# Last tiles of two experts side by side in TensorE's columns, and narrow tiles turned as 80 rows

## The chip, the core and the metric

The kernel runs on one core of a Trainium2 chip. The metric is the device time of one execution in microseconds; the time given is the median of three runs. The engines are named as in the profile: PE (TensorE), DVE (VectorE), ACT (ScalarE), POOL (GpSimd), SP (SyncE, which issues DMAs here).

## The reference

A graph layer with a mixture of experts, then a residual and a layer norm, over 12500 nodes of 256 features. Each node goes to its best 2 of 64 experts; the part of the reference around the change is this:

```python
h1 = gelu(einsum('ecd,edh->ech', h, w1) + b1[:, None, :], approximate=False)   # 256 -> 512
h2 = einsum('ech,ehd->ecd', h1, w2) + b2[:, None, :]                           # 512 -> 256
y_s = where(valid[:, None], h2.reshape(E * CAP, D)[slot], 0.0)
core = zeros((N, D)).at[tok_s].add(g_s[:, None] * y_s)                         # both experts of a node
```

`h` holds the rows of the nodes that an expert was given (at most CAP = 1024 for each), `g_s` the gate of a node for the expert. All is float32.

## The kernel before

The program has stages that follow each other: degrees and ordering of the edges, sums over edges, graph convolution and choice of experts, the experts, and the two normalisations. The change is in the stage of the experts.

**The work of the stage.** The experts are ordered by the number of their nodes, and `TOKENS` holds for each place in that order a bound in units of 16 rows. `parts` cuts each expert's rows into parts of at most four tiles of 128 rows (P); the last tile of an expert may have 16, 32, 48, 64, 80, 96 or 112 rows. There are 83 parts: the smallest expert first, then the others from the largest down.

**One part q.** Its steps, with the lines of the profile:

- `begin(q)`: when the part is an expert's first, registers are loaded with the expert's number, the expert's table of rows is copied (`tables`, L1762), and `load` issues the DMAs of its weights on SP (`w`, L1614, 1026 KB, and `bb`); `gather` (L1638) then issues on POOL one indirect DMA per tile, which fetches the rows into `xg` (16 buffers). The weights have three buffers.
- `turned(q)`: `gates_of` (L1682, DVE) makes the gates from two further columns of the gathered rows; `turn` transposes the tiles on PE into `xtp` (L1653) and copies them on DVE to `xT` (L1658).
- `hidden(q)`: eight matmuls `hp` (L1667) and four Gelu on ACT (L1671).
- `outputs(q)`: for each tile four matmuls into `yp` (L1694; two PSUM buffers), each with a tile of `h1` as the stationary operand, so that a tile of r rows uses r of PE's 128 columns. In the trace each float32 matmul shows as two records, a transpose as one. DVE adds the bias (L1699) and multiplies by the gate (L1700) into `yo` (six buffers), and POOL issues the indirect DMA that adds the rows to `z_d` (L1701). Scatter-adds of one expert are declared free of each other; one of another expert waits for the landing of those before it.

**What sets the order.** PE's order is the program's (`manual_schedule` for PE): hidden(q), transposes of part q+1, products of part q. Gathers are called three parts ahead (`AHEAD`). On the other engines a scheduler places the instructions, by priorities of its own; each engine then works through its queue in order.

```python
h1 = hidden(given[i][0], xT, m)
if q + AHEAD < len(parts):
    begin(q + AHEAD)
if q + 1 < len(parts):
    xT = turned(q + 1)
outputs(*given[i], table(q), gate.pop(q), h1, m, f"expert{i}")
```

Of the kernel before, what the change touches and what calls it, by code (L numbers as in the profile page):

```python
# [8 lines left out]
F32 = mybir.dt.float32  # L9
# [5 lines left out]
ALU = mybir.AluOpType  # L15
# [4 lines left out]
P = 128  # L20
N = 12500
D = 256
H = 512
E = 64
# [72 lines left out]
def last_node(g):  # L97
# [12 lines left out]
]  # L110
RPE = CAP // P
NSLOT = E * RPE
WROW = 2 * H + 4 * D + 4
# [8 lines left out]
def gnn_moe_kernel(  # L122
# [1478 lines left out]


    with ExitStack() as stack:
        wp = stack.enter_context(tc.tile_pool(name="w", bufs=3))
        one = stack.enter_context(tc.tile_pool(name="x_one", bufs=1))
        two = stack.enter_context(tc.tile_pool(name="x_two", bufs=2))
        ps1 = stack.enter_context(tc.tile_pool(name="x_ps1", bufs=1, space=PSUM))
# [11 lines left out]
        def overfull():  # L1619
# [8 lines left out]
            V.tensor_reduce(some, room, axis=AX.X, op=ALU.add)  # L1628
            V.tensor_copy(over_n, some)

        def gather(at, m):

            xg = []
            for k in range(0, m, P):
                r = min(P, m - k)
                k //= P
                g = two.tile([P, D2], F32, name="xg", bufs=16)
                GP.indirect_dma_start(  # L1638
                    out=g[:r],
                    out_offset=None,  # L1640
                    in_=x2_d,
                    in_offset=bass.IndirectOffsetOnAxis(ap=at[:r, 0, k : k + 1], axis=0),
                )
                xg.append(g[:r])
            return xg

        def turn(xg):

            xtp = ps1.tile([P, 2, 4 * P], F32, name="xtp")
            for k, g in enumerate(xg):  # L1650
                r = g.shape[0]
                for c in range(2):
                    T.transpose(  # L1653
                        xtp[:, c, k * P : k * P + r], g[:, c * P : (c + 1) * P], ident[:r, :r]
                    )
            m = k * P + r
            xT = two.tile([P, 2, 4 * P], F32, name="xT")
            V.tensor_copy(xT[:, :, :m], xtp[:, :, :m])  # L1658
            return xT
# [17 lines left out]
        def gates_of(xg, second):  # L1677
# [7 lines left out]
                )  # L1685
            return gate

        def outputs(w, bb, at, gate, h1, m, group):
            w2 = w[:, 2 * H : 2 * H + 4 * D].rearrange("p (c d) -> p c d", d=D)
            for k in range(-(-m // P)):  # L1690
                r = min(P, m - k * P)
                yp = ps2.tile([P, D], F32, name="yp")
                for j in range(4):
                    T.matmul(  # L1694
                        yp[:r], h1[:, j, k * P : k * P + r], w2[:, j],
                        start=j == 0, stop=j == 3,
                    )
                yo = two.tile([P, D], F32, name="yo", bufs=6)
                V.tensor_add(yo[:r], yp[:r], bb[:r])  # L1699
                V.tensor_scalar_mul(yo[:r], yo[:r], gate[:r, k : k + 1])  # L1700
                st = GP.indirect_dma_start(  # L1701
                    out=z_d,
                    out_offset=bass.IndirectOffsetOnAxis(
                        ap=at[:r, 1, k : k + 1], axis=0
                    ),
                    in_=yo[:r],
                    in_offset=None,
                    compute_op=ALU.add,
                )
                if group:  # L1710
                    tc.declare_no_dep(st.ins, group=group, reason="no node has an expert twice")
                    tc.add_to_no_dep_group(group, st.ins)


        parts = []
        for i in [E - 1, *range(E - 1)]:
            n = -(-TOKENS[i] * TU // P)
            k = -(-n // 4)
            b = 0
            for j in range(k):  # L1720
                m = (n - b + k - j - 1) // (k - j)
                parts.append((i, b, min(m * P, TOKENS[i] * TU - b * P)))
                b += m
        AHEAD = 3
        xg, given = {}, {}

        def begin(q):
            i, b, m = parts[q]
            if b == 0:
                k = 0 if i == E - 1 else i % REGS  # L1730
                if k == 0:
                    n = 1 if i == E - 1 else min(REGS, E - 1 - i)
# [14 lines left out]
                    given["regs"] = regs, columns  # L1747
                regs, columns = given["regs"]
                columns_of[i] = columns[k]
                sort_slots(i, 0)  # L1750
                if q >= AHEAD:
                    sort_slots(i, 1)
                given[i] = load(regs[k])
            xg[q] = gather(table(q), m)

        columns_of = {}

        def sort_slots(i, which):

# [6 lines left out]
        def table(q):  # L1766
            i, b, m = parts[q]
            return sorted_[:, :, i * RPE + b : i * RPE + b + 4]

        def turned(q):  # L1770
            i, b, m = parts[q]
            gate[q] = gates_of(xg[q], snd_sorted[:, i * RPE + b : i * RPE + b + 4])
            return turn(xg.pop(q))

        gate = {}
        snd_sorted = one.tile([P, NSLOT], F32)
        with tc.manual_schedule(engines={mybir.EngineType.PE}):
            for q in range(AHEAD):
# [6 lines left out]
            for q, (i, b, m) in enumerate(parts):  # L1785
                if q >= 6 and q % 4 == 2 and (q - 6) // 4 < len(LOADS):
                    t0, n = LOADS[(q - 6) // 4]
                    r = rows(t0)
                    nc.sync.dma_start(xs[:r, t0 : t0 + n], part_of(x, t0, n))
                h1 = hidden(given[i][0], xT, m)  # L1790
                if q + AHEAD < len(parts):
                    begin(q + AHEAD)
                if q + 1 < len(parts):
                    xT = turned(q + 1)
                outputs(*given[i], table(q), gate.pop(q), h1, m, f"expert{i}")
                if q == 16:
                    overfull()


        with tc.If(nc.values_load(over_n[0:1, 0:1]) > 0):  # L1800
# [5 lines left out]
            with tc.For_i(0, E, 1) as e:  # L1806
# [5 lines left out]
                for b in range(0, RPE, 4):  # L1812
                    ab = at[:, :, b : b + 4]
                    g = gather(ab, 4 * P)
                    gb = gates_of(g, second[:, b : b + 4])
                    outputs(w, bb, ab, gb, hidden(w, turn(g), 4 * P), 4 * P, None)


    with ExitStack() as stack:
# [191 lines left out]
```

## Time and profile before

| | |
|---|---|
| median of three runs | 3584.51 us (3563.84 to 3585.21) |
| the profiled execution's own time | 3578.72 us |
| its span, first to last instruction | 3576.8 us |
| mean granted PE clock over the span | 0.829 |
| busy, share of the span | PE 71%, DVE 50%, ACT 22%, POOL 61% |
| matmuls `yp` (L1694) | 1928 records, 436.3 us busy |
| matmuls `hp` (L1667) | 1328 records, 392.3 us busy |
| gathers `xg` (L1638) on POOL | 241, mean 972 ns |
| scatter-adds `z_d` (L1701) on POOL | 241, mean 1556 ns |

The busy share is an average over stages with different limits. In a row of a group, the numbers behind the count are busy time and the mean duration of one instruction; matmuls overlap, so that the mean of one is longer than the distance between two. A row in order of time gives start, length, engine, line, operation, count, and in brackets how long the engine had been idle and what ended that. L numbers are lines of the kernel.

### The profile page before, as it was taken

How to read it: one execution, taken by the hardware profiler on the slowest of the kernel's cores; microseconds unless marked ns; L12 is line 12 of the kernel's file. 1: busy time of each engine (PE TensorE's matmuls, PEld its weight loads, DVE VectorE, ACT ScalarE, POOL GpSimd, SP SyncE). 2: the span in 40 equal slices, each digit the busy share in tenths (PEclk: the TensorE clock that was granted, in tenths of full speed). 3: DMA queues.
4: the chain of work that ended last, by engine and by line, in shares of the span. 5: the costliest groups of instructions: out<-in, count | busy, mean ns of one | idle time of the engine just before them, and what ended most of it. 6: DMA issues, size and time to landing. Idle time of an engine off the chain costs nothing. (4 is left out here: it accounts for less than half of the span.)

```text
span 3576.8 us, 40049 instructions
## 1 busy us (share of the span) xinstructions
PE 2531.0 (71%) x11797; PEld 1893.4 (53%) x11797; DVE 1800.6 (50%) x7368; ACT 798.8 (22%) x1975; POOL 2175.5 (61%) x2095
## 2 busy tenths in 40 slices
PE   2526075566776667676766666677699999999966
PEld 2415043455555555554555444454377876677856
DVE  3729454355555465655555435467543333333358
ACT  2416301122111122212221111111111221122246
POOL 7250776666666666666666666665367777777610
PEclk6657566778887878897878777788899999999988
DMA  8450853444554555555544444444555666676764
GB/s 259 128 189 6 309 203 95 158 145 144 143 150 146 141 147 168 146 147 157 155 144 122 142 117 122 119 135 124 159 115 122 134 135 146 155 177 173 197 196 144
DMA packets 313919, 538.03 MB, mean 150 GB/s; under 512 B 47274, under 2 KB 233102, under 8 KB 305502
## 3 DMA queue, kind: packets, MB, share of 16 engines
q0 software_dynamic: 119360, 266.30, 28.9%
q1 hardware_dynamic: 180795, 256.19, 23.0%
q10 hardware_dynamic: 13539, 12.90, 1.2%
q8 instruction: 97, 1.59, 0.2%
q14 instruction: 128, 1.05, 0.1%
HBM read 431.02 MB, written 105.28 MB: 150 GB/s over the span
## 5 line engine op out<-in xcount | busy, mean ns | idle before, releaser
L938 POOL DMA_INDIRECT ring<-h_d,src_col x1416 | 1372.4, 969 | 711.8 <-issue 387.2
L952 PE MATMUL p<-ring,o 128*128 128x258 f32 x2832 | 902.0, 450 | 213.2 <-issue 89.7
L952 PEld LDWEIGHTS p<-ring,o 128*128 128x128 f32 x2832 | 600.4, 224 | 389.2 <-issue 214.9
L930 DVE TENSOR_SCALAR o<-lane,rel 128x128 f32<-128x128 f32 x1416 | 356.1, 297 | 402.7 <-remote 160.3
L1701 POOL DMA_INDIRECT z_d<-yo,tables x241 | 375.0, 1556 | 129.8 <-issue 58.0
L1694 PE MATMUL yp<-w,h 128*128 128x256 f32 (+7 forms) x1928 | 436.3, 381 | 0.8 <-DVE tables L1762 0.8
L1667 PE MATMUL hp<-xT,w 128*128 128x384 f32 (+22 forms) x1328 | 392.3, 449 | 9.4 <-issue 9.4
L1694 PEld LDWEIGHTS yp<-w,h 128*128 128x128 f32 (+7 forms) x1928 | 336.8, 179 | 71.0 <-issue 7.6
L1638 POOL DMA_INDIRECT xg<-x_d,tables x241 | 234.3, 972 | 183.7 <-PE xtp L1653 88.2
L1671 ACT ACTIVATE h<-hp,w 128x384 f32<-128x384 f32 (+21 forms) x332 | 178.7, 539 | 682.0 <-PE hp L1667 673.1
L1667 PEld LDWEIGHTS hp<-xT,w 128*128 128x128 f32 x1328 | 248.0, 192 | 134.1 <-issue 61.0
L1506 ACT ACTIVATE again<-again,factor 128x256 f32<-128x256 f32 x180 | 82.4, 501 | 670.3 <-issue 363.2
L986 ACT COPY s<-p 128x258 f32<-128x258 f32 x118 | 43.8, 371 | 814.8 <-PE p L952 450.0
L1658 DVE COPY xT<-xtp 128x672 f32<-128x672 f32 (+21 forms) x83 | 70.8, 853 | 305.6 <-PE xtp L1653 297.2
L1699 DVE TENSOR_TENSOR yo<-yp,bb 128x256 f32<-128x256 f32 (+7 forms) x241 | 102.0, 423 | 224.1 <-PE yp L1694 154.2
L285 POOL DMA_INDIRECT early<-in_x,src_col x130 | 135.0, 1038 | 102.4 <-DMA early_d<-early 56.3
L567 PE MATMUL deg<-o_hi,o_lo 128*128 128x98 bf16 x1254 | 107.3, 254 | 122.8 <-issue 83.8
L1481 PE MATMUL q<-r_out,tables 128*128 128x98 f32 x360 | 66.8, 315 | 150.4 <-DVE tables L1489 55.9
L1027 PE MATMUL q<-ident,s 128*128 128x128 f32 x236 | 58.9, 337 | 158.0 <-DVE tables L1489 67.5
L222 DVE TENSOR_TENSOR o_hi<-lane_b,hi 128x2450 bf16<-128x2450 bf16 (+1 forms) x67 | 95.1, 1419 | 145.8 <-remote 106.2
L565 ACT ACTIVATE s_lo<-lane_b,nb 128x128 bf16<-128x128 bf16 x396 | 121.8, 388 | 192.9 <-remote 126.7
L567 PEld LDWEIGHTS <-o_lo 128*128 128x128 bf16 x1254 | 87.5, 125 | 140.1 <-issue 91.2
(367 smaller groups left out, 3503.5 us busy)
## 6 DMA issues: line engine op xcount, KB each, us to landing
w<-in_wpack SPq DMA_DIRECT2D x64, 1026.0 KB
again<-early_d SPq DMA_DIRECT2D x90, 256.0 KB
ring<-h_d,src_col POOLq DMA_INDIRECT x1416
early_d<-early SPq DMA_DIRECT2D x65, 256.0 KB
tables<-h_d SPq DMA_DIRECT2D x104, 128.0 KB
acc<-acc_d SPq DMA_DIRECT2D x14, 896.0 KB
acc<-in_x SPq DMA_DIRECT2D x12, 1024.0 KB
x_d<-y SPq DMA_DIRECT2D x47, 258.0 KB
```

Source lines behind the costliest of these rows:

```text
L285: GP.indirect_dma_start(out=t[:, c % 2], out_offset=None, in_=x, in_offset=bass.IndirectOffsetOnAxis(ap=src_col[:, MC + c : MC + c + 1], a ...
L565: S.activation(s_lo[:, i], lane_b, AF.Sign, bias=nb[:, k - k0, i : i + 1])
L567: T.matmul(deg, o_lo[:, i], o_hi[:, i], start=c + i == 0, stop=False)
L930: o_last[u] = V.tensor_scalar(o_of[u][:, j], lane, rel[:, c : c + 1], None, op0=ALU.is_equal)
L938: i = GP.indirect_dma_start(out=r[:, k, :D], out_offset=None, in_=h_d, in_offset=bass.IndirectOffsetOnAxis(ap=src_col[:, c : c + 1], axis=0),)
L952: i = T.matmul(p_of[g], o_of[v][:, n], r[:, k], start=j == 0, stop=j == GR - 1)
L1638: GP.indirect_dma_start(out=g[:r], out_offset=None, in_=x2_d, in_offset=bass.IndirectOffsetOnAxis(ap=at[:r, 0, k : k + 1], axis=0),)
L1667: T.matmul(hp[:, :m], w1[:, c, j * P : (j + 1) * P], xT[:, c, :m], start=c == 0, stop=c == 1,)
L1671: S.activation(h1[:, j, :m], hp[:, :m], AF.Gelu, bias=w[:, 2 * H + 4 * D + j : 2 * H + 4 * D + j + 1],)
L1694: T.matmul(yp[:r], h1[:, j, k * P : k * P + r], w2[:, j], start=j == 0, stop=j == 3,)
L1699: V.tensor_add(yo[:r], yp[:r], bb[:r])
L1701: st = GP.indirect_dma_start(out=z_d, out_offset=bass.IndirectOffsetOnAxis(ap=at[:r, 1, k : k + 1], axis=0), in_=yo[:r], in_offset=None, c ...
```

## The change

Of the experts whose last tile has at most 64 rows (`SIDE`), each is paired with the next such expert (`PAIR_OF`): eleven pairs. The second of a pair is moved directly behind the first, and its parts are reversed, so that the two parts that hold the last tiles follow each other. The first of these two parts computes its full tiles only and keeps its last tile's operands. At the second part, `pair_of_outputs` puts both last tiles into one `yp` tile, the first at rows 0 and the second at row 64, and alternates their matmuls: one of the first, one of the second, four times. Only then does `begin(q + AHEAD)` run, with its gathers pinned in program order, and the second part's full tiles come behind the last of these gathers.

A tile of fewer than 80 rows (`WHOLE`) is gathered and transposed as 80 rows; the copy to `xT` still takes only the part's own rows. The weights have four buffers, and the registers are loaded in groups that follow the new order.

```diff
+SIDE = P // 2
+WHOLE = SIDE + 16
+PAIR_OF = {}
+for _i, _n in enumerate(TOKENS[: E - 2]):
+    if 0 < _n * TU % P <= SIDE:
+        _open = [_k for _k, _v in PAIR_OF.items() if _v is None]
+        PAIR_OF.update({_open[0]: _i} if _open else {_i: None})
+PAIR_OF = {_k: _v for _k, _v in PAIR_OF.items() if _v is not None}
...
-        wp = stack.enter_context(tc.tile_pool(name="w", bufs=3))
+        wp = stack.enter_context(tc.tile_pool(name="w", bufs=4))
...
-                r = min(P, m - k)
+                r = max(WHOLE, min(P, m - k))
...
+                if last_gather.get("pin"):
+                    tc.keep_in_program_order(i)
+                last_gather["i"] = i.ins
...
+        def pair_of_outputs(two_of):
+
+            yp = ps2.tile([P, D], F32, name="yp")
+            sides = [yp[i * SIDE : i * SIDE + m % P] for i, (_, _, _, _, _, m, _) in enumerate(two_of)]
+            for j in range(4):
+                for side, (w, bb, at, gate, h1, m, group) in zip(sides, two_of):
+                    products(side, m % P, w, h1, m // P * P, j)
+            for i, (side, (w, bb, at, gate, h1, m, group)) in enumerate(zip(sides, two_of)):
+                r = m % P
+                add_to_nodes(
+                    side, r, bb[i * SIDE : i * SIDE + r], at, gate, m // P, group
+                )
...
+        order = [E - 1]
+        for i in range(E - 1):
+            if i not in order:
+                order += [i, *([PAIR_OF[i]] if i in PAIR_OF else [])]
...
+            parts += of[::-1] if i in PAIR_OF.values() else of
+        pair_at = {}
+        for q, (i, b, m) in enumerate(parts[1:], 1):
+            if PAIR_OF.get(parts[q - 1][0]) == i:
+                assert 0 < m % P <= SIDE and 0 < parts[q - 1][2] % P <= SIDE
+                pair_at[q] = q - 1
...
-                if q + AHEAD < len(parts):
+                if q not in pair_at and q + AHEAD < len(parts):
                     begin(q + AHEAD)
                 if q + 1 < len(parts):
                     xT = turned(q + 1)
-                outputs(*given[i], table(q), gate.pop(q), h1, m, f"expert{i}")
+                mine = (*given[i], table(q), gate.pop(q), h1, m, f"expert{i}")
+                if q in pair_at:
+                    pair_of_outputs([kept.pop(pair_at[q]), mine])
+                if q in pair_at or q in pair_at.values():
+                    if q not in pair_at:
+                        kept[q] = mine
+                    mine = (*mine[:5], m // P * P, mine[6])
+                if q in pair_at:
+                    last_gather["pin"] = True
+                    begin(q + AHEAD)
+                    last_gather["pin"] = False
+                    with tc.issue_after(last_gather["i"]):
+                        outputs(*mine)
+                else:
+                    outputs(*mine)
```

`products` holds the matmul of `outputs`, and `add_to_nodes` its add, multiplication and scatter-add, both as they were.

More of the change, by code (lines that the diff above doesn't have):

```diff
@@ L1629, in overfull @@
             V.tensor_copy(over_n, some)
+        last_gather = {}
         def gather(at, m):
@@ L1693, in outputs @@
                 for j in range(4):
[L1694 to L1708, printed above, removed]
-                )
-                if group:
-                    tc.declare_no_dep(st.ins, group=group, reason="no node has an expert twice")
-                    tc.add_to_no_dep_group(group, st.ins)
+                    products(yp[:r], r, w, h1, k * P, j)
+                add_to_nodes(yp[:r], r, bb[:r], at, gate, k, group)
+        def pair_of_outputs(two_of):
[8 more added lines that the diff above has]
+                    side, r, bb[i * SIDE : i * SIDE + r], at, gate, m // P, group
+                )
+        order = [E - 1]
+        for i in range(E - 1):
+            if i not in order:
+                order += [i, *([PAIR_OF[i]] if i in PAIR_OF else [])]
         parts = []
-        for i in [E - 1, *range(E - 1)]:
+        for i in order:
             n = -(-TOKENS[i] * TU // P)
```

50 lines of the change are left out of this document (33 added, 17 removed).

## The prediction

> **What bounds the kernel now.** I read the page first, then PE's waits and busy time in the stretch of the experts, then the chain that ended last, then the three queues (PE, DVE, POOL) in order of time.
>
> ```profile
> span 3576.8 us, 40049 instructions
> PE 2531.0 (71%) x11797; PEld 1893.4 (53%) x11797; DVE 1800.6 (50%) x7368; ACT 798.8 (22%) x1975; POOL 2175.5 (61%) x2095
> ...
> 2562.00:3429.00 867.00, 857.13 (x3734) 638.63 (x3734) 318.12 (x985) 180.00 (x333) 599.54 (x473) 0.99 0.65 151
> ...
> PE hp L1667 <- issue: 9.4, 2, 8.8
> PE yp L1694 <- DVE tables L1762: 0.8, 1, 0.8
> ```
>
> The change touches only the stage of the experts, from 2562 to 3429 us: the built programs of before and after hold the same instructions in the same order ahead of it and behind it. In this stage the columns of the window are PE, PEld, DVE, ACT, POOL: PE is busy 857.13 of 867 us, and its waits sum to 10.2 us, all at the start. So a microsecond that PE saves here is a microsecond of the kernel, and a wait put on PE costs its full length. POOL is busy 599.54 us (69%), DVE 318 us (37%).
>
> ```profile
> 3430.93 1.53 POOL z_d L1701
> ...
> 3432.79 3.70 DMA z_d<-yo,tables
> 3436.51 0.37 SPq L1852
> ```
>
> The chain says how the stage ends: the last scatter-add into z_d is issued at 3432.79, lands 3.70 us later, and only then do the loads of the next stage start. A late POOL at the end is on the path too.
>
> **Why PE never waits now: POOL's lead.**
>
> ```profile
> POOL xg L1638 <- PE xtp L1653: 87.3, 63, 2.5
> DVE gate L1682 <- DMA xg<-x_d,tables: 4.0, 6, 1.0
> ...
> 3185.78 0.94 POOL L1638 DMA_INDIRECT xg<-x_d,tables  x1 [0.30 <-issue]
> 3187.02 1.00 POOL L1638 DMA_INDIRECT xg<-x_d,tables  x1 [0.30 <-issue]
> 3188.32 1.64 POOL L1701 DMA_INDIRECT z_d<-yo,tables  x1 [0.30 <-issue]
> 3190.26 1.57 POOL L1701 DMA_INDIRECT z_d<-yo,tables  x1 [0.30 <-DVE yo L1699]
> 3192.14 1.46 POOL L1701 DMA_INDIRECT z_d<-yo,tables  x1 [0.30 <-issue]
> ...
> 3190.66 0.47 DVE L1682 SCALAR_TENSOR_TENSOR gate<-snd_sorted,xg 128x1 f32<-128x1 f32 x3
> 3195.15 0.89 DVE L1658 COPY xT<-xtp 128x704 f32<-128x704 f32 x1 [4.02 <-PE xtp L1653]
> 3196.91 0.42 DVE L1699 TENSOR_TENSOR yo<-yp,bb 128x256 f32<-128x256 f32 x1 [0.86 <-DMA z_d<-yo,tables]
> ```
>
> POOL's gathers mostly wait for a free xg buffer (87.3 us): POOL runs as far ahead as sixteen buffers allow. Therefore the gates on DVE, which read the gathered rows, find them landed: 4.0 us of waiting in the whole stage, all at its start. This matters because the scheduler puts gates early in DVE's queue: in the built program of before, behind the adds of part q stand the gates of part q+4, and only then the xT copy of part q+2 and the yo adds of part q+1. DVE works in order, so a gate whose rows are late holds that copy and those adds.
>
> **The change, part by part.**
>
> *Gathers behind the pair (the costliest edit).* For the eleven parts that end a pair, begin(q+3) is called after the pair's outputs, its gathers are pinned in program order, and the remaining outputs come after them. The scheduler kept the early gates. Around the first pair (parts 12 and 13; gN is the gates of part N, XN its xT copy) the built queues read:
>
> ```
> POOL: S12.2  S13.2  G16 x3  S13.0 S13.1  G17 x2  G18 x3  G19 x3  S14.0
> DVE:  X14  +12.2 +13.2 *12.2 *13.2  +13.0 +13.1 (*)  g16 x3  g17 x2  X15  +14.0
> PE:   pair 12|13, 13.0 13.1, hidden 14, turn 15, 14.0 14.1 14.2
> ```
>
> Before, G16 and G17 stood ahead of S11. Now they stand behind S13.2, while g17 still stands ahead of +14.0. PE has two yp buffers, so product 14.2 waits for +14.0. From the end of the pair on PE: adds and multiplications until S12.2 can go 1.4 us (three DVE rows of 0.35 to 0.42 and the signals); S13.2 is of another expert than S12.2 and waits for its landing, s; then POOL's issue spacing, 1.88 us for a scatter and 1.27 for a gather (from the rows above). For s:
>
> ```profile
> 3213.19 1.43 POOL L1701 DMA_INDIRECT z_d<-yo,tables  x1 [0.31 <-issue]
> ...
> 3221.22 1.63 POOL L1701 DMA_INDIRECT z_d<-yo,tables  x1 [1.83 <-DMA z_d<-yo,tables]
> ...
> 2552.15 1.11 POOL L1638 DMA_INDIRECT xg<-x_d,tables  x1 [40.81 <-DVE tables L1762]
> ...
> 2559.72 0.22 DVE L1682 SCALAR_TENSOR_TENSOR gate<-snd_sorted,xg 128x1 f32<-128x1 f32 x1 [6.54 <-DMA xg<-x_d,tables]
> ```
>
> s is bounded by 3.7 us (the chain, little traffic) and 7.7 (3213.19 to the end of the wait before 3221.22); I take 5.0, since the pair's end frees a weight buffer and so starts a 1 MB load at that moment. A gather's landing after POOL's part of it is bounded by 0 and 6.5 us (2553.26 to 2559.72, three weight loads under way); I take 2.3, what the chain's scatter shows (3.70 less its 1.44 on POOL).
>
> Sum for this pair: 1.4 + 5.0 + 1.88 (S13.2) + 3 x 1.27 + 2 x 1.88 + 2 x 1.27 - 0.3 + 2.3 = 20.4, and gate, X15 and +14.0 with signals 1.7: 22.1 us. PE in that time has two products tiles 3.46, hidden(14) 5.16, turn 0.65, two tiles 3.46 (rows below): 12.7. Stall: 9.4 us. With n gathered tiles, r remaining tiles, and PE's hidden+turn h, the stall is 8.5 + 1.27 n + 0.15 r - h, less 0.9 where the copy isn't behind the gates:
>
> | pair ends with part | n | r | h | stall |
> |---|---|---|---|---|
> | 13 | 5 | 2 | 5.8 | 9.4 |
> | 17 | 5 | 1 | 5.8 | 8.3 |
> | 35 | 6 | 1 | 5.8 | 9.6 |
> | 39 | 8 | 3 | 7.8 | 11.4 |
> | 46 | 7 | 3 | 6.4 | 11.5 |
> | 48 | 6 | 3 | 6.0 | 10.6 |
> | 50 | 6 | 2 | 5.8 | 10.6 |
>
> Together 71 us. For the last four pairs (64, 66, 68, 70), which follow each other, three gathers stand ahead of the copy X(q+2): 1.4 + 5.0 + 1.88 + 3.8 - 0.3 + 2.3 + 1.3 = 15.4 against 3.46 + 4.1 + 0.6 + 3.46 = 11.6 on PE: 3.8 us; and, in the first three, the next gates hold the adds that free yp, some 2.7 us more. Together 22 us. No engine hides this: PE is the bound.
>
> *What an idle PE does to its clock.*
>
> ```profile
> 2576.00:2580.00 4.00, 0.20 (x1) 0.51 0.41 101
> ...
> 2579.80 8.67 PE L1667 MATMUL hp<-xT,w 128*128 128x512 f32 x16 [8.76 <-issue]
> ...
> 2969.37 7.13 PE L1667 MATMUL hp<-xT,w 128*128 128x512 f32 x16
> ```
>
> After the one idle time of 8.76 us the granted clock (the third number from the right in a row of the window, here 0.51) was half, and sixteen matmuls took 8.67 instead of 7.13 us: 1.5 us. Seven stalls of this length: +10.5 us (bounds 0 and 15).
>
> *PE's own savings.* Each row starts where PE began the group; the time to the next row's start is its cost.
>
> ```profile
> 2885.90 0.52 PE L1653 MATMUL xtp<-ident,xg 128*128 128x128 f32 x4
> 2886.26 5.38 PE L1694 MATMUL yp<-w,h 128*128 128x256 f32 x24
> 2891.48 2.98 PE L1667 MATMUL hp<-xT,w 128*128 128x208 f32 x16
> ...
> 2894.95 3.62 PE L1694 MATMUL yp<-w,h 128*128 128x256 f32 x16
> 2898.41 5.32 PE L1667 MATMUL hp<-xT,w 128*128 128x384 f32 x16
> 2903.57 0.65 PE L1653 MATMUL xtp<-ident,xg 128*128 128x128 f32 x4
> 2904.14 5.45 PE L1694 MATMUL yp<-w,h 128*128 128x256 f32 x24
> 2909.43 2.76 PE L1667 MATMUL hp<-xT,w 128*128 128x192 f32 x16
> ...
> 2948.14 3.74 PE L1694 MATMUL yp<-w,h 128*128 128x256 f32 x16
> 2951.80 5.43 PE L1667 MATMUL hp<-xT,w 128*128 128x384 f32 x16
> 2957.07 0.60 PE L1653 MATMUL xtp<-ident,xg 128*128 128x128 f32 x4
> ```
>
> Turning 128+80 rows and the products behind it took 0.36 + 5.22 us, 128+64 rows 0.57 + 5.29: a tile of up to 64 rows costs 0.28 us more than one of 80. 24 such tiles are now turned as 80 rows: -6.7 us. Products of 128+80 rows took 3.46 us and the hidden layer behind them 5.16; of 128+32 rows 3.66 and 5.27: a narrow tile costs 0.31 us for going into PE's narrow columns and out. A record of a product costs 3.46/16 = 0.216 us, and each matmul is two.
>
> No row shows two products side by side. In the built program, five pairs keep one column width (two at 64 columns, three at 32); six alternate between a 64-wide and a 32-wide tile at every matmul. For the five, if the second record of one side overlaps the first of the other, 16 records take 9 slots: 7 x 0.216 = 1.51 saved, and one way in and out, 0.31: 1.82 each, -9.1. Bounds: 0.31 (no overlap) and 1.82. For the six I take that each of the seven inner changes of width costs half of 0.31: +1.05 - 0.31 = +0.74 each, +4.4. Bounds: +0.74 and -1.82. I choose the upper end because the only changes of width that the trace has all cost time. PE's own: -6.7 - 9.1 + 4.4 = -11.4.
>
> The Trainium skill, "TensorEngine Tiling (Array Packing)", Key Properties, says that a change of the tiling mode, not merely of the tile, drains TensorE. By it the six pairs gain nothing; without it all eleven would overlap, and this term would be -27 instead of -11.4. The trace has the change between 128 and 32 or 64 columns alone, not that between 64 and 32.
>
> *The stage's end.* Behind the last pair the built POOL queue has nine gathers ahead of S71.0: 11.4 us late; ten parts of two scatters then need about 5.7 us each on POOL (2 x 1.88 and the landing) against some 6.7 on PE, so most is made good: +4 us (0 to 11).
>
> *At nothing:* the 944 further rows that are gathered (POOL's time is per instruction), the register loads for the reordered experts (SP and DVE have room), the weight load that begin(q+3) also issues (on SP it waits for its buffer before and after), and the fourth weight buffer (PE never waited for w; the loads start a part earlier).
>
> Sum: 71 + 22 + 10.5 - 11.4 + 4 = +96 us on the profiled execution's own time, 3578.72 us (span 3576.8 and 1.9 around it): **3674 us**. That execution is 5.8 us under the median of the runs, well within their spread.
>
> **The rivals.**
> 1. *POOL's lead suffices* (not slower). If the gathers of q+3 and q+4 land before g(q+4) holds anything, no stall arises; 4.0 us of gate waits now speak for it, the queue above against it. It needs 9 us less per pair, more than s and both landings at their least give back (some 4). Then only PE's own counts: -11 to -27, 3552 to 3567 us.
> 2. *All eleven pairs overlap* (the six too): -27 instead of -11.4, 3658 us.
> 3. *The change doesn't do what it says: none overlaps.* The five lose 1.51 each: 3682 us.
> 4. *Slow landings:* s at 7.7 and gathers at 5 us under the weight loads: 11 x (2.7 + 2.7) more, 3733 us.
>
> **How the numbers follow.** Forecast 0.54, rival 1 0.10, rival 2 0.12, rival 3 0.10, rival 4 0.12; 0.02 is left for a gain that I don't see. Range: s at 3.7 takes 14 us off, gather landings at nothing 25, no clock loss 10, rival 2 15; nearly all of it: 3614 us. Upwards s and landings at two thirds of rival 4, with no overlap, and the median above the profiled execution: 3728 us. A measurement of this kernel tells about 1% (36 us) from no change. Faster by more needs more than all that PE can save: 0.02. Within 1% is rival 1: 0.10. Slower is the forecast with the three others: 0.88.
>
> **What would show it.** Right: PE's waits in the stage hold yp on DVE seven times at 8 to 12 us and hp on DVE's xT near the end, gates on DVE wait for the gathers some 100 us, and POOL's scatter waits 2 to 6 us on z_d eleven times. The granted clock halves behind each. Wrong: gates that don't wait, or yp records of a six-pair that start together. The forecast falls if PE stays busy over 95% of the stage.

## The result, and the profile after

The changed kernel takes 3700.31 us in the median of six runs (3684.30 to 3709.65), the kernel before 3576.98 us in the runs beside it. The ratio is 1.036, with a 95% interval of 1.031 to 1.041: the change costs about 123 us.

The page of the changed kernel, its span and its busy times:

```profile
span 3682.5 us, 40034 instructions
PE 2554.4 (69%) x11797; PEld 1911.4 (52%) x11797; DVE 1800.8 (49%) x7368; ACT 798.9 (22%) x1975; POOL 2187.6 (59%) x2095
```

The work is the same to within a per cent, and yet the span is 105.7 us longer, so the time went into waiting. Windows by stage of the changed kernel, and in a second block the earlier stages of the one before (the columns behind the length are the busy times of PE, PEld, DVE, ACT and POOL, the granted clock, the DMA share and GB/s):

```profile
0.00:2534.00 2534.00, 1587.64 (x7373) 1180.34 (x7373) 1373.55 (x6046) 524.37 (x1467) 1585.37 (x1619) 0.76 0.51 150
2534.00:3537.00 1003.00, 878.10 (x3738) 648.52 (x3738) 319.91 (x996) 179.80 (x333) 599.22 (x475) 0.94 0.58 132
3537.00:3682.00 145.00, 88.66 (x686) 82.53 (x686) 107.37 (x327) 94.77 (x175) 2.98 (x2) 0.84 0.56 179
```

```profile
0.00:2559.00 2559.00, 1583.86 (x7373) 1171.90 (x7373) 1373.37 (x6046) 524.00 (x1467) 1570.91 (x1618) 0.77 0.49 148
```

PE's stage of the experts, from its first transposition to its last product, took 869.0 us before and takes 1002.5 now: 133.5 more. The stages ahead of it, which the change doesn't touch, were 25.6 us shorter in this execution; that is why the spans differ by less than the stage does, and why the experiments below are read by the stage.

What PE waits for in the stage, and what DVE and POOL wait for (total, number of times, longest; `...` marks rows left out, here and below):

```profile
PE yp L1702 <- DVE yo L1706: 61.5, 12, 12.1
PE hp L1679 <- DVE xT L1670: 26.3, 4, 7.6
PE yp L1702 <- issue: 20.1, 9, 12.2
...
PE yp L1702 <- ACT h L1683: 5.8, 1, 5.8
...
DVE gate L1694 <- DMA xg<-x_d,tables: 191.1, 67, 12.8
...
POOL xg L1648 <- PE xtp L1666: 37.4, 31, 3.2
POOL z_d L1708 <- DMA z_d<-yo,tables: 19.7, 7, 5.8
```

PE's waits were 10.2 us behind the stage's first transposition; now those four kinds alone are 113.7. ("issue" names no releaser; the one wait of 12.2 us among these nine ends, like the others, right behind late gates and an add on DVE.) DVE's gates wait 191 us for gathered rows, where they waited 4. POOL waits for a free xg buffer 37 us instead of 87: it has lost its lead.

The first pair (parts 12 and 13) in order of time:

```profile
2717.52 1.43 POOL L1708 DMA_INDIRECT z_d<-yo,tables  x1 [7.76 <-DVE yo L1707]
...
2722.43 1.35 POOL L1708 DMA_INDIRECT z_d<-yo,tables  x1 [3.48 <-issue]
2724.08 1.01 POOL L1648 DMA_INDIRECT xg<-x_d,tables  x1 [0.30 <-issue]
...
2726.95 0.22 DVE L1694 SCALAR_TENSOR_TENSOR gate<-snd_sorted,xg 128x1 f32<-128x1 f32 x1 [6.49 <-DMA xg<-x_d,tables]
2727.91 1.64 POOL L1708 DMA_INDIRECT z_d<-yo,tables  x1 [0.30 <-issue]
...
2731.75 1.02 POOL L1648 DMA_INDIRECT xg<-x_d,tables  x1 [0.30 <-issue]
2733.07 0.95 POOL L1648 DMA_INDIRECT xg<-x_d,tables  x1 [0.30 <-issue]
...
2734.70 0.22 DVE L1694 SCALAR_TENSOR_TENSOR gate<-snd_sorted,xg 128x1 f32<-128x1 f32 x1 [4.65 <-DMA xg<-x_d,tables]
...
2736.13 0.21 DVE L1694 SCALAR_TENSOR_TENSOR gate<-snd_sorted,xg 80x1 f32<-80x1 f32 x1 [1.22 <-DMA xg<-x_d,tables]
2736.27 0.95 DVE L1670 COPY xT<-xtp 128x768 f32<-128x768 f32 x1
...
2737.14 0.41 DVE L1706 TENSOR_TENSOR yo<-yp,bb 128x256 f32<-128x256 f32 x1
...
2737.60 3.78 PE L1702 MATMUL yp<-w,h 128*128 128x256 f32 x8 [8.72 <-DVE yo L1706]
```

Read from the top: the scatter-add of part 12's last tile, then part 13's, held until the first has landed, 4.9 us behind it (the row says "issue", but POOL's sequencer waits there for the semaphore, the signal of landing, of the first one's DMA, whose last update came at 2721.68). Then the three gathers of part 16, part 13's full tiles, and the gathers of part 17 at 2731.75 and 2733.07. Their gates on DVE come at 2734.70 and 2736.13. Behind these gates in DVE's queue stand the xT copy and the add that frees the yp buffer, and PE's product starts right behind that add, 8.7 us idle. The chain is the one of the built queue.

Behind the stop the clock is down; a window that begins inside the stop has a granted clock of 0.51 (third number from the right), and the mean of the whole stage fell from 0.99 to 0.94:

```profile
2731.00:2741.00 10.00, 3.40 (x8) 2.78 (x9) 2.67 (x7) 0.00 (x0) 7.56 (x9) 0.51 0.45 94
```

### The profile page after: what moved, and what is told of

Same layout as the page of the kernel before. It is cut to its first block, busy times and chain, and to the rows that moved or that the text cites. A ratio compares the mean times of both kernels' runs of the same rounds, so it can differ in the third digit from the quotient of the medians.

```text
span 3682.5 us, 40034 instructions
## 1 busy us (share of the span) xinstructions
PE 2554.4 (69%) x11797; PEld 1911.4 (52%) x11797; DVE 1800.8 (49%) x7368; ACT 798.9 (22%) x1975; POOL 2187.6 (59%) x2095
## 5 line engine op out<-in xcount | busy, mean ns | idle before, releaser
L960 PEld LDWEIGHTS p<-ring,o 128*128 128x128 f32 x2832 | 608.1, 227 | 375.8 <-issue 182.1
L1702 PE MATMUL yp<-w,h 128*128 128x256 f32 (+7 forms) x1928 | 454.3, 394 | 87.5 <-DVE yo L1706 61.5
L1679 PE MATMUL hp<-xT,w 128*128 128x384 f32 (+22 forms) x1328 | 398.8, 455 | 36.2 <-DVE xT L1670 26.3
L1683 ACT ACTIVATE h<-hp,w 128x384 f32<-128x384 f32 (+19 forms) x332 | 178.5, 539 | 815.2 <-PE hp L1679 712.8
L1706 DVE TENSOR_TENSOR yo<-yp,bb 128x256 f32<-128x256 f32 (+6 forms) x241 | 101.8, 423 | 213.4 <-PE yp L1702 166.7
L1670 DVE COPY xT<-xtp 128x768 f32<-128x768 f32 (+18 forms) x83 | 70.7, 852 | 261.4 <-PE xtp L1666 207.2
L293 POOL DMA_INDIRECT early<-in_x,src_col x130 | 144.8, 1114 | 77.3 <-issue 36.9
L1489 PEld LDWEIGHTS q<-r_out,tables 128*128 128x128 f32 x360 | 63.6, 232 | 188.6 <-issue 75.0
L1313 PE MATMUL tab<-at,vals 128*128 128x512 bf16 x392 | 135.4, 433 | 29.2 <-DVE vals L1299 17.2
L1497 DVE SCALAR_TENSOR_TENSOR tables<-lane,high,q 128x98 f32<-128x98 f32 x180 | 49.8, 314 | 197.2 <-remote 112.8
```

Source lines behind the costliest of these rows:

```text
L293: GP.indirect_dma_start(out=t[:, c % 2], out_offset=None, in_=x, in_offset=bass.IndirectOffsetOnAxis(ap=src_col[:, MC + c : MC + c + 1], a ...
L960: i = T.matmul(p_of[g], o_of[v][:, n], r[:, k], start=j == 0, stop=j == GR - 1)
L1313: T.matmul(tab, vals[:r, m], at[:r], start=entered[0] + m == 1, stop=entered[0] + m == 2 * NT + 1,)
L1489: T.matmul(p_r[:, i], wide[:, i * P : (i + 1) * P], r_out, start=True, stop=True)
L1679: T.matmul(hp[:, :m], w1[:, c, j * P : (j + 1) * P], xT[:, c, :m], start=c == 0, stop=c == 1,)
L1683: S.activation(h1[:, j, :m], hp[:, :m], AF.Gelu, bias=w[:, 2 * H + 4 * D + j : 2 * H + 4 * D + j + 1],)
```

## The experiments

All numbers of stages are from the one profiled execution of each kernel. "PE's stage" runs from its first transposition to the end of its last product; "last scatter-add" is the start of POOL's last one, counted from the same first transposition. The ratio is against the kernel before on the same chip; it is of the whole program, and how far a stage differs between two executions of one kernel isn't on record. The edits are shown shortened. "12 yo" means twelve yo buffers instead of six, "equal" pairs of one column width, "early" the gathers early.

| kernel | ratio (95%) | PE's stage, us | last scatter-add, us |
|---|---|---|---|
| before | 1 | 869.0 | 873.0 |
| changed | 1.036 (1.031 to 1.041) | 1002.5 | 1005.8 |
| gathers early | 1.004 (1.0005 to 1.0075) | 884.8 | 901.0 |
| gates late | 1.018 (1.012 to 1.025) | 944.1 | 947.6 |
| gathers between | 1.028 (1.020 to 1.035) | 968.9 | 970.3 |
| equal widths | 1.035 (1.028 to 1.042) | 1009.0 | 1010.5 |
| gates late, 12 yo | 1.020 (1.013 to 1.026) | 930.7 | 938.4 |
| changed, 12 yo | 1.043 (1.036 to 1.050) | 1009.3 | 1010.8 |
| early, 12 yo | 1.005 (1.001 to 1.009) | 860.2 | 892.1 |
| early, 12 yo, equal | 1.007 (1.003 to 1.011) | 844.2 | 874.4 |
| the same, gathers in the landing | 1.004 (1.000 to 1.008) | 883.0 | 892.6 |
| before, narrow tiles halved | 0.998 (0.994 to 1.001) | 850.8 | 853.7 |
| early, 12 yo, equal, not alternating | 1.004 (1.000 to 1.008) | 855.0 | 887.9 |
| early, 12 yo, equal, seven pairs | 0.995 (0.9936 to 0.9964) | 847.3 | 855.4 |

**Gathers early.** Does the place of the gathers make the loss, or the pairs?

```diff
-                if q not in pair_at and q + AHEAD < len(parts):
-                    begin(q + AHEAD)
+                if q + AHEAD < len(parts):
+                    begin(q + AHEAD, late=q in pair_at)   # late: without the load of w
...
-                    begin(q + AHEAD)                       # behind the pair, pinned
+                    given[i] = load(reg_of[i])             # i: the expert of part q + AHEAD
```

> The changed kernel, but at a pair the gathers of the part three further on are issued at the usual place, ahead of the pair; only the load of its weights waits until the pair is done (a one-element memset on POOL keeps the full tiles' scatter-adds behind the pair's). Theory: the loss is the late gathers, which hold DVE's queue and through it the yp buffer. Then the waits of PE's products on DVE's adds (61.5 us in 12 waits after the change) and of the hidden layer on the xT copy (26.3 in 4) fall to under 5 us, DVE's gates wait for xg under 10 us instead of 180, PE's own gain stays (6.7 from the 80-row turning, 5 equal-width pairs at about 2 us less each, 6 mixed pairs at 0.7 more each), and the time is 3563 us, 12 to 14 below before (ratio 0.994 to 1.000). Rival, the pairs themselves cost it (the two tiles drain the array or wait for each other): it stays over 1.02.

The stage falls from 1002.5 to 884.8 us: 118 of the 133.5 us are due to where eleven parts' gathers stand. The rival is out. But the forecast of 12 to 14 us below the kernel before failed: this one is slower by 0.4%. Two rows of its waits, PE's and DVE's, and DVE's in the kernel before:

```profile
PE yp L1703 <- DVE yo L1707: 19.8, 7, 5.1
...
DVE yo L1707 <- DMA z_d<-yo,tables: 78.9, 34, 6.3
```

```profile
DVE yo L1699 <- DMA z_d<-yo,tables: 12.1, 14, 1.1
```

DVE's adds now wait 79 us for a yo buffer whose scatter-add hasn't landed (12.1 us before the change), and four times, at the last pairs or behind them, that reaches PE.

**Gates late.** The gathers stay late; only DVE's order is changed.

```diff
-            gate[q] = gates_of(xg[q], ...)
-            return turn(xg.pop(q), m)
+            tiles = xg.pop(q)
+            xT = turn(tiles, m)
+            with tc.issue_after(last_gather["xT"]):        # the copy to xT
+                gate[q] = gates_of(tiles, ...)
+            return xT
```

> The changed kernel, gathers as late as there, but in DVE's queue a part's gates stand behind that part's own xT copy instead of some parts ahead. Theory: DVE's order is what turns the late gathers into a stall, since the gathers of part q+3 are needed by PE only after two more parts (20 to 24 us after a pair of the first seven). Then the seven stalls of 7.8 to 12.6 us go (70 us together, and 10 us of half clock behind them); of the last four, whose parts are half as long, 0 to 20 us stay. Time 3568 to 3600, ratio 0.997 to 1.007. Rival, POOL's lateness itself is the wait and any order on DVE only moves it: the stalls stay above half, ratio over 1.018.

The time lies between theory and rival. The stage loses 58 of its 133 extra us, and the stop of the first pair is gone; but 60 us more than before remain in PE's stops:

```profile
PE yp L1702 <- ACT h L1683: 24.0, 7, 8.1
PE xtp L1666 <- DMA xg<-x_d,tables: 17.7, 15, 3.3
```

What holds the Gelu of the first row isn't shown. The second row is plain: at the short parts the transposes themselves now wait for the late gathers. So changing DVE's order gives back somewhat less than half of the loss; the lateness of the gathers hurts without it too.

**Gathers between.** DVE's order as in the changed kernel, but the gathers stand between the pair's two scatter-adds.

```diff
             for i, (side, ...) in enumerate(zip(sides, two_of)):
+                if i:
+                    begin(then)          # part q + AHEAD, pinned here
                 add_to_nodes(side, ...)
```

> The changed kernel with DVE's order as it is there, but the gathers of the part three further on stand between the pair's two scatter-adds on POOL, so that they no longer wait for the first one's landing (4.6 to 4.9 us at the first pair). Theory: the landing is one term of each stall, of 5 us; with it gone the seven stalls fall from 70 us to some 30 (where the part after that is held too by a gather behind the second scatter-add, 4 us go instead of 5), the last four from 28 to some 10. Time 55 us below the changed kernel, ratio to before about 1.02 (1.01 to 1.026). Rival, POOL's own time per instruction and not the landing sets the stall: under 15 us gained, ratio over 1.03.

The stage loses 34 us, of the 55 expected; the waits of the products on DVE's adds fall from 61.5 to 39.5 us. PE's idle time at the seven first pairs falls from 67.4 to 42.5 us, the waits of the hidden layer at the last four from 26.3 to 17.8. So each of the seven gives back 3.6 us of a landing of some 5: the landing is a term of each stall, though less comes of it than forecast (some 30 and 10 us were to be left).

**Equal widths.** Pairs are drawn only within a width.

```diff
-        _open = [_k for _k, _v in PAIR_OF.items() if _v is None]
+        _open = [_k for _k, _v in PAIR_OF.items() if _v is None
+                 and (TOKENS[_k] * TU % P <= P // 4) == (_n * TU % P <= P // 4)]
```

> The changed kernel with eleven pairs drawn only among tiles of up to 32 rows or only among tiles of 48 and 64 (before: six of eleven mix the two). Theory: a pair of equal width runs its 16 products in 8 slots (1.55 us from first to last start), a mixed one takes 4.2 us as each change of width empties the array; so PE's products shrink by 6 times 2.6 = 16 us, while the seven stalls stay at 60 to 75 us. Time 10 to 20 us below the changed kernel, ratio to before 1.028 to 1.034. Rival, the width change costs nothing of the time because PE waits behind these products anyway: the stalls grow by what the products lose, and the time is that of the changed kernel within 5 us.

Here the theory fell. The products shrink as forecast (each of the eleven pairs costs 1.94 to 1.98 us; the rows are below), and the stage is no shorter, 1009.0 us: PE's idle time in it grew from 135 to 149 us. That fits the rival, by which PE waits out what it saves, though the stage is 6.5 us longer than the changed kernel's, not within 5.

```profile
PE yp L1705 <- DVE yo L1709: 56.2, 9, 12.0
...
PE yp L1705 <- DVE xT L1673: 19.1, 2, 9.9
```

**Twelve yo buffers**, in the kernel with the gates late, in the changed one, and in the one with the gathers early:

```diff
-            yo = two.tile([P, D], F32, name="yo", bufs=6)
+            yo = two.tile([P, D], F32, name="yo", bufs=12)
```

> The kernel with the gates late once more, with twelve buffers of yo instead of six. In that one the stage still stood 75 us above before (944.1 against 869.0), in stops of 4 to 8.5 us ahead of products, while POOL ran eight gathers in one row ahead of the next scatter-adds. Theory: the late gathers do harm in a second way; bunched behind the pair they delay the scatter-adds behind them, the six yo buffers fill, DVE's next add waits for one, and PE's next products for that add. With twelve, PE's waits ahead of products (51.7 us in 18) fall below 12, the turnings' waits for xg (17.7 in 15) stay: the stage is 895 to 912 us, the ratio to before 1.004 to 1.012. Rival, the products wait for something that the ring doesn't touch: the stage stays over 930, the ratio over 1.015.

> The changed kernel with twelve buffers of yo instead of six, nothing else. Theory, two ways of which DVE's order is the larger: at the first pair three gates wait 6.5, 4.7 and 1.2 us for xg ahead of the adds, whatever the ring; so the seven stalls keep 55 to 70 of their 70 us, and only the small pauses (14 us) and a part of the last four go. Stage 960 to 990 us (1002.5 with six), ratio to before 1.022 to 1.034. Rival, the ring alone is the cause: the stalls go, ratio under 1.01.

> The kernel with the gathers early, with twelve buffers of yo instead of six. With six its stage was 884.8 us, with 17.8 us of four stops ahead of products at the last pairs, where DVE's add waits up to 6.3 us for a scatter-add six tiles back to land. Theory: with twelve these stops and the half clock behind them go, PE's own gain of 10 us shows, and the stage is 858 to 866 us, the ratio 0.995 to 1.000. Rival, POOL's chain of scatter-add and landing is itself as slow as PE there, and the ring only puts the stop off: over 875 us, ratio over 1.001.

In the first the theory fell, and the rival held: 13 of 75 us, and the ratio is what it was. The stops that remain stand behind xT copies that start long after their transposes, such as this one, whose transposes began at 3184.68:

```profile
3190.28 0.96 DVE L1670 COPY xT<-xtp 128x768 f32<-128x768 f32 x1 [9.74 <-PE yp L1702]
```

The row names a PE product that PE had done more than a microsecond earlier; what holds such a copy stays open. In the changed kernel the ring does nothing at all (1009.3 us): the gates hold the queue, whatever the buffers, and the small pauses stay too. In the third PE's stage is 860.2, as expected, and yet the time is 0.5% over before. Where it went, in PE's waits behind the stage, in this run and in the kernel before:

```profile
PE q L1918 <- DMA tables<-z_d: 39.8, 1, 39.8
```

```profile
PE q L1863 <- DMA tables<-z_d: 11.9, 1, 11.9
```

PE is done early, and the next stage waits for POOL's last scatter-add, which starts 892.1 us after the stage's start, later than before the change. The buffers only let the delay pile up unseen.

**With equal widths on top**, all that PE can save:

> The same (gathers early, twelve yo buffers), with the eleven pairs drawn among tiles of up to 32 rows or among tiles of 48 and 64, as in the run where this saved 25 us of products and no time. Theory: there the stalls took it back; with the stalls gone the products count. A pair of equal width costs 1.96 us beside full tiles, as one narrow tile alone does, a mixed one 4.6, so 15 to 16 us less than the run with early gathers and twelve buffers: stage 843 to 851 us, 18 to 26 below before, ratio 0.991 to 0.996. Rival, another engine (POOL) sets the pace of these parts by now: within 5 us of that run.

PE's stage is 844.2 us, 25 below before, as forecast; the time is not. POOL's last scatter-add starts at 874.4 us, where it was 873.0. The rival of this run, POOL's pace, holds. Its ratio of 1.007 is more than these 1.4 us account for; where the rest lies isn't shown (in the one profiled execution the stages behind the last scatter-add take 143 us, against 144 before).

Why POOL is late here: the two parts of one of the last pairs on POOL, then SP's weight loads in that time, and, for comparison, a stretch of the kernel without pairs in which the narrow tiles run half of their products (next run):

```profile
3251.11 1.49 POOL L1712 DMA_INDIRECT z_d<-yo,tables  x1 [0.30 <-issue]
3255.19 1.40 POOL L1712 DMA_INDIRECT z_d<-yo,tables  x1 [2.59 <-issue]
...
3256.90 1.58 POOL L1712 DMA_INDIRECT z_d<-yo,tables  x1 [0.27 <-DVE xT L1674]
3258.78 1.57 POOL L1712 DMA_INDIRECT z_d<-yo,tables  x1 [0.30 <-issue]
...
3267.05 1.62 POOL L1712 DMA_INDIRECT z_d<-yo,tables  x1 [2.84 <-DVE xT L1674]
...
3274.72 1.43 POOL L1712 DMA_INDIRECT z_d<-yo,tables  x1 [0.30 <-DVE xT L1674]
```

```profile
3257.97 0.33 SPq L1625 DMA_DIRECT2D w<-in_wpack  x1
...
3261.62 0.33 SPq L1625 DMA_DIRECT2D w<-in_wpack  x1
```

```profile
3239.05 1.44 POOL L1702 DMA_INDIRECT z_d<-yo,tables  x1 [0.30 <-issue]
3240.79 1.01 POOL L1638 DMA_INDIRECT xg<-x_d,tables  x1 [0.30 <-PE yp L1695]
3242.11 0.88 POOL L1638 DMA_INDIRECT xg<-x_d,tables  x1 [0.30 <-issue]
3243.30 0.97 POOL L1638 DMA_INDIRECT xg<-x_d,tables  x1 [0.30 <-issue]
3244.60 1.62 POOL L1702 DMA_INDIRECT z_d<-yo,tables  x1 [0.33 <-issue]
...
3254.51 1.62 POOL L1702 DMA_INDIRECT z_d<-yo,tables  x1 [0.86 <-DMA z_d<-yo,tables]
```

Without pairs, an expert's last scatter-add (3239.05) is followed by three gathers, and when they are issued it has landed: the next expert's scatter-add waits 0.33 us, and a part takes POOL 9.4 to 9.9 us. In a pair the two last tiles are scattered one right behind the other, so that the landing between them has no gathers in it (2.59 us idle), and the scatter-add at 3267.05 starts 6.7 us after POOL is done with the second part's last one, for whose landing it waits, while two weight loads run. From 3251.11 to 3274.72 two parts take 23.6 us; PE does them in 18 (its pairs begin at 3237.56, 3255.92, 3273.84 and 3291.42). POOL's first scatter-add of the pair comes 13.6, 18.8, 23.4 and 29.6 us behind these starts: it falls back by some 5 us from each of the last four pairs to the next. How much of that is the pair's order on POOL, and how much the two weight loads beside the landing, isn't separated.

**Half of the narrow products, no pairs.** The kernel before, in which tiles of up to 64 rows leave out two of their four products. Is POOL as tight as that without any pair?

```diff
-                for j in range(4):
+                of = 2 if r <= P // 2 else 4
+                for j in range(of):
...
-                        start=j == 0, stop=j == 3,
+                        start=j == 0, stop=j == of - 1,
```

> The kernel before, without any pair, but the last tiles of up to 64 rows run only two of their four products (half of the hidden layer is left out for these rows). It takes about as much from PE as eleven pairs of equal width at best: 24 tiles at half of 1.96, 23 us, and moves nothing else. Theory, POOL's row of scatter-adds paces the stage as much as PE does: PE's stage falls from 869 to 850 us or less, but the last scatter-add still starts 862 to 875 us after the stage's start (873.0 before), and the ratio is 0.997 to 1.002. Rival, POOL only follows PE in the kernel before and the pairs alone lengthen its row: the last scatter-add starts at 848 to 856 us, ratio 0.992 to 0.995.

My theory fell by the stage: PE's stage is 850.8, and the last scatter-add starts at 853.7, as the rival had it. In the kernel before POOL follows PE; by the stage it is the pairs that lengthen POOL's row. The time doesn't settle it: the ratio, 0.998 (0.994 to 1.001), lies in the theory's range and not in the rival's (0.992 to 0.995), though 19 us less would be 0.995 and its interval holds that too.

**Gathers in the landing.** The gathers of the part four further on stand between the pair's two scatter-adds.

```diff
                 if i:
+                    begin(then, late=True)   # then: part q + AHEAD + 1, pinned here
                 add_to_nodes(side, ...)
```

> Gathers early, twelve yo buffers, pairs of equal width (stage 844.2 us, but POOL's last scatter-add starts 874.4 us after the stage's start, 30 us behind PE, as against 873.0 before), and the gathers of the part four further on now stand between the pair's two scatter-adds on POOL, in the time of the first one's landing. Theory: POOL's row of scatter-adds and landings is a second bound beside PE, and a pair lengthens it by a landing wait that nothing fills; filled, eleven waits of 2.3 to 4.6 us shrink by the 2.5 to 3.8 us of the gathers, the last scatter-add starts at 845 to 862 us, and the time is 10 to 25 us below before, ratio 0.992 to 0.998. Rival, POOL's row is bound by its own instructions, or the gathers drawn forward delay scatter-adds as in the changed kernel: the last scatter-add still starts at 868 us or later, ratio 0.999 or more.

The theory fell: the stage is 883.0 us and the last scatter-add starts at 892.6. In the built queue further gathers stand bunched behind the pinned ones once more, and DVE's gates wait again (this run, then the one without this edit):

```profile
DVE gate L1698 <- DMA xg<-x_d,tables: 91.3, 37, 8.7
```

```profile
DVE gate L1698 <- DMA xg<-x_d,tables: 9.8, 6, 6.6
```

**Not alternating.** The four products of one tile, then the four of the other.

```diff
-            for j in range(4):
-                for side, (...) in zip(sides, two_of):
+            for side, (...) in zip(sides, two_of):
+                for j in range(4):
```

> Gathers early, twelve yo buffers, pairs of equal width, but the two tiles' products don't alternate: the four of one tile, then the four of the other. Theory, only neighbouring products on different columns run side by side: a pair's 16 records take 16 slots but for the border, 3.7 to 3.9 us beside 1.96, so PE's stage is some 20 us longer than with alternation (844.2), 860 to 867 us; the time stays within 0.5% of that run, since POOL's last scatter-add (874 us) ends the stage. Rival, the array overlaps what stands on different columns in any order: stage within 4 us of 844.

Both theories were off: the stage is 855.0 us, half-way. PE's groups, each row's distance to the next row being its cost: a mixed pair and an equal one of the run with early gathers and twelve buffers, then an equal one without alternation, each with two full tiles:

```profile
2744.56 8.22 PE L1703 MATMUL yp<-w,h 128*64 128x256 f32 x32
2752.62 1.78 PE L1680 MATMUL hp<-xT,w 128*128 128x384 f32 x5
...
3303.64 5.58 PE L1703 MATMUL yp<-w,h 128*48 128x256 f32 x32
3309.06 2.35 PE L1680 MATMUL hp<-xT,w 128*128 128x288 f32 x9
```

```profile
3266.42 6.49 PE L1706 MATMUL yp<-w,h 128*48 128x256 f32 x32
3272.74 1.62 PE L1683 MATMUL hp<-xT,w 128*128 128x288 f32 x6
```

8.06, 5.42 and 6.32 us. Two full tiles are 16 records of 0.216, 3.46 us; so a mixed pair costs 4.60, an equal one 1.96, and one that doesn't alternate 2.86. A narrow tile alone costs 3.66 - 1.73 = 1.93.

**Seven pairs.** The last four pairs, where POOL falls back, are left as they were.

```diff
-for _i, _n in enumerate(TOKENS[: E - 2]):
+for _i, _n in enumerate(TOKENS[: 43]):
```

> Gathers early, twelve yo buffers, pairs of equal width, but only the first seven of the eleven pairs; the last four, among parts of two full tiles, go as before the change. Theory: beside the run with half products POOL's row of scatter-adds loses some 6 us up to its 200th scatter-add and 15 more by the 208th, where the last four pairs stand: parts so short leave POOL no idle time in which to catch up a landing. Without those four, PE gains 4.3 from the turning and 7 times 1.96, 18 us: stage 849 to 854 us, last scatter-add 855 to 864 us after the stage's start (873.0 before, 874.4 with eleven), time 10 to 20 us below before, ratio 0.994 to 0.998. Rival, the row falls behind at each pair wherever it stands: last scatter-add over 868 us, ratio 0.999 or more.

PE's stage is 847.3 us (a little below the forecast 849 to 854) and the last scatter-add starts at 855.4: the delay doesn't build up at the first seven pairs. The time is 3137.55 against 3154.89 us, 17.3 less, ratio 0.995 (0.9936 to 0.9964). This chip ran the earlier stages of the program some 400 us faster than the others. This version beats the kernel before by 0.5%; it wasn't run beside the changed one. How much of that the pairs give, and how much the 80 rows or the twelve buffers would give without any pair, wasn't run.

## Why the prediction was right, and where its sum was off

The forecast was 3674 us, slower; 3700.31 us was measured. On the stage it was +96 us, and +133.5 came. That the profiled execution of the changed kernel, 3684.30 us, is within 11 us of the forecast is luck: its earlier stages were 25.6 us shorter. By its steps (the stops are idle times of PE, as the rows show them):

- *Gathers behind the pair, first seven pairs: right in place and size.* Predicted 71 us. The seven stops are 8.7, 7.4, 8.8, 12.2, 10.0, 12.1 and 8.2 us (forecast 9.4, 8.3, 9.6, 11.4, 11.5, 10.6 and 10.6), 67.4 together. The inputs held at the first pair: 4.9 us from the first scatter-add to the second instead of 1.43 + 0.30 on POOL alone, where s was taken as 5.0; gathers landed 1.9 us behind POOL's part (2732.77 to 2734.70) where 2.3 was taken. The run with early gathers shows that this edit is the cause.
- *The last four pairs: mis-sized.* Predicted 22 us (its own terms, 4 x 3.8 and 3 x 2.7, add up to 23). The four stops ahead of the hidden layer are 4.7, 6.6, 7.6 and 7.5 where 3.8 each was forecast; of the further waits for yp 0.9 us came between them, and one stop of 5.8 behind the last pair. That is 33.0. The sum took each pair by itself; the stops grow from one to the next, as if POOL had not made up for one pair when the next came, which is argued and not shown.
- *Not foreseen: eight pauses of 0.9 to 2.4 us,* 11.9 together, beside the stalls, two of them ahead of the first pair. Such pauses stay with twelve yo buffers, so it isn't the ring; their cause is open.
- *The clock: mis-sized.* Predicted 10.5 us. PE's waits grew by 113.7 us and its own work shrank by some 12; what is left of the 133.5 is some 32 us in which records take longer than usual. The granted clock accounts for most of it: PE was busy for 62 us of the stage at a granted clock of one half (0.51 in the row above, the stop included), where it had been 8 us before; that loses 27 us. The forecast charged 1.5 us for each of seven stops, from sixteen matmuls after a single one; the four last pairs, too, and the product tiles behind each stop pay.
- *PE's own: right.* Predicted -11.4. In the run with early gathers and twelve buffers, which has the changed kernel's work on PE and hardly its stops, PE is busy 846.4 us in the stage, against 858.2 before: -11.8. Turning as 80 rows saves 0.17 to 0.22 us, and the products behind it 0.06 to 0.07, as the 0.28 of the sum had it. An equal pair costs what one narrow tile costs, 1.96 us: 16 records in 8 slots, not 9, so 5 x 1.96 = 9.8 instead of 9.1. A mixed one costs 4.55 to 4.60 where two narrow tiles cost 3.9 to 4.0, +0.6 to +0.7, as taken (+0.74). The Trainium skill, "TensorEngine Tiling (Array Packing)", Key Properties, says that a change of tiling mode drains TensorE; 4.60 against 1.96 us agrees with it, where 64 and 32 columns are two modes.
- *The stage's end.* Predicted +4; the last scatter-add starts 3.3 us behind PE's stage where it started 4.0 behind it before, so this term was nothing.
- *What the forecast did not see:* that the pairs cost twice. Of its signs, DVE's gates waited 191 us, not some 100, and the granted clock halved behind the stops as said. Had PE's stalls been taken away alone, rival 1 expected 3552 to 3567 us; the run with the gathers early, which took most of them away, is at 1.004, and with twelve buffers too at 1.005. A pair puts two scatter-adds, the second of which must wait for the first, side by side on POOL, and the landing between them has lost the gathers that covered it.

So most of the loss is shown to come from the eleven late begin(q+3). Behind them, small but enough to eat the gain, POOL's row of scatter-adds is late: at the last four pairs, since without these the delay is all but gone (855.4 against 853.7 us in the run without pairs). How much of the late gathers' harm comes through DVE's order isn't settled; gates late gave back 58 us, and some of what stayed has no known releaser.

## What to carry to other kernels

When work of two iterations is joined, look at everything that now has to wait for the join, and move only what must: here one weight load had to wait, and eleven parts' gathers were moved with it. An engine that runs ahead lends its lead to all in-order queues behind it; a gate placed early costs nothing while the rows are there and stops a whole queue once they aren't. And before joining two outputs, ask whether the writes that follow had been kept apart by something useful.

## What was not expected of the hardware

- Products of two tiles on different columns of one width overlap fully when they alternate (1.96 us for 16 records, as for 8), and still in part when they don't (2.86; one behind the other, 16 records of 0.216 would be 3.46).
- A scatter-add had landed 3.75 us after its start on POOL for the last one of the run with eleven equal pairs; where two 1 MB weight loads were issued beside it, the next one, which waits for it, started 8.3 us after its start (3258.78 to 3267.05).
- In the run with seven pairs the stages ahead of the experts took 2140 us on that chip, against 2532 to 2601 in the other experiments and in the two kernels; PE's stage of the experts, 847.3 us, was within 4 us of what runs with about the same work on PE took elsewhere (844.2 and 850.8).
